# A graph attention kernel: deviation by Ln and Exp from one table set, and another split of the neighbour rows over the engines

## The chip, the cores and the metric

The kernel runs on one core of one Trainium2 chip. The core has TensorE (PE), VectorE (DVE), ScalarE (ACT), GpSimd (POOL) and the DMA queues, of which SP's and POOL's are used most here. Each engine takes its instructions in order; the engines wait for each other through semaphores. The time is device microseconds per execution. The kernel before takes 5428.85 us, the median of 3 runs (5423.94 to 5437.06).

## The reference

Two graph attention layers over 10,000 nodes and 170,000 edges (each node also has a loop of its own), each with layer norm and a residual, and one more layer norm at the end, all in float32:

```python
def gat_conv(x, edge_index, W, a_src, a_dst, bias, heads, out_ch, concat):
    ...
    xl = (x @ W).reshape(n, heads, out_ch)
    alpha_src = jnp.einsum('nhc,hc->nh', xl, a_src)
    alpha_dst = jnp.einsum('nhc,hc->nh', xl, a_dst)
    e = jax.nn.leaky_relu(alpha_src[src] + alpha_dst[dst], 0.2)
    m = jax.ops.segment_max(e, dst, num_segments=n)
    e = jnp.exp(e - m[dst])
    s = jax.ops.segment_sum(e, dst, num_segments=n)
    alpha = e / (s[dst] + 1e-16)
    out = jax.ops.segment_sum(xl[src] * alpha[:, :, None], dst, num_segments=n)
    ...
def layer_norm(x, g, b):
    ...
    return (x - mu) * jax.lax.rsqrt(var + LN_EPS) * g + b
h = layer_norm(gat_conv(x, ..., W1, ..., HEADS, HID, True), g1, be1)
h1 = jax.nn.relu(h) + (x @ Wr1 + br1)
h = layer_norm(gat_conv(h1, ..., W2, ..., 1, OUT_DIM, False), g2, be2)
y = h + (h1 @ Wr2 + br2)
x = _layernorm(x + y)
```

Layer 1 has 4 heads of 256 columns, layer 2 one head of 768.

## The kernel before

First it computes x @ W1 for all 79 tiles of 128 nodes, writes it to a table in memory, one row of 1033 numbers a node, and sorts the nodes by their number of neighbours meanwhile. `TURNS` is the order in which the sorted tiles are worked: first every other tile from few neighbours to many, then back. So a tile has `SLOTS[t]` rows, from 8 up to 27 and one of 41 in the middle, and down to 9. A "row" in this text is such a slot: for each of the tile's 128 nodes one neighbour's table row, gathered by one POOL DMA into a ring in SBUF (29 rows in layer 1, 41 in layer 2).

**Layer 1** (`ordered_layer1`, L679) works tile by tile, in an order written out by hand:

- `logits` (L472) adds and subtracts on DVE and takes Exp on ACT (L486), for all rows of a tile; `normalised` (L493) divides by the sum on DVE. `weights_of` (L733) issues both, the next tile's while this tile is still being summed (the last `EARLY` = 5 rows, later where the ring is too small; for tiles of 24 rows or more only after the tile).
- The rows are summed by their weights in three ways. The first `on_pe(t)` rows go to PE: ACT makes a diagonal matrix for each head (L722), PE multiplies it with the row (L728). Every `SHARE`-th of the others is multiplied and added by DVE alone (four instructions, L520). The rest are shared: ACT multiplies in place (L509, four instructions, `multiply`), DVE adds (L516, one instruction).
- The diagonals of a tile are issued in two halves, two rows and the remaining ones; between them ACT's order has the deviation of the tile before.
- `deviation` (L569) takes the mean and variance on DVE (L573, L575) and a Sqrt on ACT (L577). `scaled` (L580) takes the reciprocal (L588) and scales on DVE (L586, L589); L799 adds the residual.
- PE turns x and h (L700), ACT copies both out of PSUM (L701), PE multiplies with Wr1 (L172) and W2 (L816), ACT copies the result for layer 2's table (L758).
- ACT's multiplies of a tile are issued ahead of DVE's sums, and all of them before the next tile's Exp.

**Layer 2** (`ordered_layer2`, L869) sums the first 512 columns of every row on DVE (L520) and the last 256 on PE (diagonals L928, matmuls L929), adds the residual product (L940, L943), and takes two norms a tile in `norms` (L948), the second with a reciprocal of its own (L956) and an Identity on ACT (L960). POOL writes the output (L962).

Sqrt and Exp are in different table sets, so the compiler puts an ACT_TABLE_LOAD before a Sqrt that follows an Exp and before an Exp that follows a Sqrt. There is a third path, `general_path`, for graphs that do not fit; it does not run here.

Of the kernel before, what the change touches and what calls it, by code (L numbers as in the profile page):

```python
# [31 lines left out]
AF = mybir.ActivationFunctionType  # L32
# [17 lines left out]
EARLY = 5  # L50
DIAGONALS = 5
ON_PE2 = 512
SHARE = 4
ON_PE1 = 4


# [24 lines left out]
def gnn_kernel(ctx, tc, x, x_cols, src, dst, src_col, dst_col, W1, a_src1, a_dst1, b1, g1, be1, Wr1, br1,  # L81
               W2, a_src2, a_dst2, b2, g2, be2, Wr2, br2, out, n_edges):
    nc = tc.nc
# [12 lines left out]
    SLOTS = CAPS  # L96
# [34 lines left out]
    eps = consts.tile([P, 1], F32, name="eps")  # L131
# [391 lines left out]
    def attend_parts(small, ring, acc, h_, ad, bias, heads, dh, t, summed=None):  # L523
# [7 lines left out]
        for lo, hi in zip(cuts, cuts[1:]):  # L531
# [25 lines left out]
            for q in range(lo, hi):  # L557
                shared = heads > 1 and (q - lo) % SHARE
                if shared:
# [5 lines left out]
    def pieces(a, width):  # L565

        return [a[:, c:c + width] for c in range(0, a.shape[1], width)]

    def deviation(small, parts):  # L569

        st = small.tile([P, len(parts), 6], F32, name="st")
        for j, a in enumerate(parts):
            nc.vector.bn_stats(st[:, j, :], a)  # L573
        mv = small.tile([P, 2], F32, name="mv")
        nc.vector.bn_aggr(mv, st.rearrange("p k s -> p (k s)"))  # L575
        sd = small.tile([P, 1], F32, name="sd")
        nc.scalar.activation(sd, mv[:, 1:2], AF.Sqrt, bias=eps)  # L577
        return mv[:, 0:1], sd

    def scaled(to, parts, mean_and_deviation, g, b):  # L580

        mean, inv = mean_and_deviation
        c = 0
        for a in parts:
            d = c + a.shape[1]
            nc.vector.scalar_tensor_tensor(to[:, c:d], a, mean, g[:, c:d], op0=OP.subtract, op1=OP.mult)  # L586
            c = d
        nc.vector.reciprocal(inv, inv)  # L588
        nc.vector.scalar_tensor_tensor(to, to, inv, b, op0=OP.mult, op1=OP.add)  # L589

    def load(s, w):
# [82 lines left out]
    SLOTS, FIRST = [SLOTS[t] for t in TURNS], [FIRST[t] for t in TURNS]  # L674

    def nodes(t):
        return order[:, TURNS[t]:TURNS[t] + 1]

    def ordered_layer1():  # L679
        with tc.tile_pool(name="b1", bufs=1) as pool, tc.tile_pool(name="small1", bufs=2) as small, \  # L680
                tc.tile_pool(name="ps_acc1", bufs=2, space=PSUM) as ps_acc, \
                tc.tile_pool(name="ps_h1", bufs=2, space=PSUM) as ps_half, \
# [30 lines left out]
            def on_pe(t):  # L713


                return min(max(SLOTS[t] // 2 - 5, 1), ON_PE1, SLOTS[t])

            def summed(acc, diagonals, e, q, lo, hi, m):

# [25 lines left out]
            def shared(t, k):  # L745
                return (k - on_pe(t)) % SHARE > 0

# [19 lines left out]
            for t in range(NT + 1):  # L767
                live, events = t < NT, []
                n = SLOTS[t] if live else 0
                first = done = on_pe(t) if live else 0  # L770
                whole = live and n <= ring.size

# [7 lines left out]
                if last:  # L780
                    r_before, means = last
                    stats = deviation(small, pieces(means[:, :C1], BANK))
# [13 lines left out]
                if last:  # L796
                    h = pool.tile([P, C1], F32, name="h")
                    scaled(h, [means[:, :C1]], stats, g1_b, be1_b)
                    nc.vector.scalar_tensor_tensor(h, h, 0.0, r_before[:, :C1], op0=OP.max, op1=OP.add)  # L799
# [69 lines left out]
    def ordered_layer2():  # L869
        nonlocal ps_big  # L870
        with tc.tile_pool(name="b2", bufs=1) as pool, tc.tile_pool(name="small2", bufs=2) as small, \
# [76 lines left out]
            def norms(t, h, r, means):  # L948

                stats = deviation(small, [a for m in means for a in pieces(m, C2 - ON_PE2)])  # L950
                yield
                scaled(h, means, stats, g2_b, be2_b)
                nc.vector.tensor_add(h, h, r[:, :C2])
                mean, inv = deviation(small, pieces(h, C2 // 2))
                yield
                nc.vector.reciprocal(inv, inv)  # L956
                less = small.tile([P, 1], F32, name="less")
                nc.vector.scalar_tensor_tensor(less, mean, -1.0, inv, op0=OP.mult, op1=OP.mult)
                o = pool.tile([P, C2], F32, name="out")
                nc.scalar.activation(o, h, AF.Identity, bias=less, scale=inv)  # L960
                yield
                nc.gpsimd.indirect_dma_start(  # L962
                    out=out, out_offset=bass.IndirectOffsetOnAxis(ap=nodes(t), axis=0),
                    in_=o, in_offset=None, bounds_check=N - 1, oob_is_err=False)
# [7 lines left out]
            for t in range(NT):  # L972
# [4 lines left out]
                if not whole(t):  # L977
# [3 lines left out]
                    nc.vector.tensor_add(ad, ring.slot(FIRST[t])[:, C2:C2 + H2], lift)  # L981
                    attend_parts(small, ring, h, h, ad, b2_b, H2, DH2, t)
                    last = norms(t, h, rs[t], [h])
                else:
                    e = (ready or list(weights_of(t)))[0]
# [22 lines left out]
                    if not t:  # L1008
                        nc.vector.tensor_add(be2_b, be2_b, adds[1])
                        nc.vector.tensor_add(be2_b, be2_b, q[:, :C2])  # L1010
                    last = norms(t, h, rs[t], [acc, rs[t][:, C2:2 * C2 - ON_PE2]])
                if t + 2 < NT and t + 2 not in ins:
                    ins[t + 2] = fetch_x(t + 2)
# [220 lines left out]
    with tc.If(all_fits > 0) as fit:  # L1234
        ordered_layer1()
        ordered_layer2()
# [49 lines left out]
```

## Time and profile before

| | |
|---|---|
| Median of 3 runs | 5428.85 us |
| Profiled execution, its own time | 5437.06 us |
| Its span | 5435.3 us |
| Mean granted TensorE clock | 0.94 |
| PE busy | 4792.7 us, 88% |
| DVE busy | 4311.7 us, 79% |
| ACT busy | 3150.6 us, 58% |
| POOL busy | 3225.8 us, 59% |
| DMA | 1591.40 MB, 293 GB/s over the span |

The page cuts the span into 40 equal slices of 136 us. One digit is the busy share in tenths, 9 for 90% or more:

```profile
PE   8999996999999886578999999999998775789998
DVE  5784244889988887688889998779988767789998
ACT  3434344788888877678888877534443332334443
PEclk9999998999999988789999999999998887889999
DMA  4333626899999997689999998599999988999995
```

The first seven slices are the table and the sorting, the next 19 layer 1, the rest layer 2. The dip in the middle of each layer is the stretch of tiles with many rows. ACT is busiest in layer 1, where it does the multiplies. A share of busy time is a mean over a stretch; whether an engine has room is read from the order of its instructions and what each waited for. In the timelines the columns are start, duration, engine, line, operation, tile written and tiles read, their shapes, the number of instructions merged into the line, and in brackets the idle time before it with what ended it.

### The profile page before, as it was taken

To read this page: it belongs to the slowest core of one execution; us is meant where nothing else is said; L and a number is where in the kernel's file an instruction comes from. 1 tells how busy PE (TensorE), PEld (TensorE's weight loads), DVE (VectorE), ACT (ScalarE), POOL (GpSimd) and SP (SyncE) were. 2 spreads that over 40 slices of the span, in tenths; PEclk is the share of its full clock that TensorE was granted. 3 is DMA by queue.
4 is the path that set the end of the run, shared out by engine and by line. 5 is a ranking of instruction groups with operands and counts; after the bars stand their busy time and mean duration, and the time that the engine had idled before them with its cause. 6 is when DMAs were issued, how large, how long until landed. Compare 5 with 4: busy or idle time off the path is not lost. (4 is left out here: it accounts for less than half of the span.)

```text
span 5435.3 us, 59962 instructions
## 1 busy us (share of the span) xinstructions
PE 4792.7 (88%) x15191; PEld 2873.3 (53%) x15191; DVE 4311.7 (79%) x7966; ACT 3150.6 (58%) x8255; POOL 3225.8 (59%) x3159
## 2 busy tenths in 40 slices
PE   8999996999999886578999999999998775789998
PEld 3444443555555544345555555566666554566665
DVE  5784244889988887688889998779988767789998
ACT  3434344788888877678888877534443332334443
POOL 3446465455665654556656655277777657677774
PEclk9999998999999988789999999999998887889999
DMA  4333626899999997689999998599999988999995
GB/s 155 124 96 90 95 92 232 288 317 346 356 348 341 349 330 283 235 318 346 352 337 347 353 335 305 178 376 378 374 363 353 325 274 306 332 348 366 369 384 216
DMA packets 474309, 1591.40 MB, mean 293 GB/s; under 512 B 118327, under 2 KB 122487, under 8 KB 473958
## 3 DMA queue, kind: packets, MB, share of 16 engines
q0 software_dynamic: 322384, 1286.62, 65.5%
q1 hardware_dynamic: 149520, 297.43, 15.9%
q10 hardware_dynamic: 2054, 3.42, 0.2%
q8 instruction: 128, 2.10, 0.2%
q14 instruction: 223, 1.83, 0.1%
HBM read 1431.80 MB, written 177.29 MB: 296 GB/s over the span
## 5 line engine op out<-in xcount | busy, mean ns | idle before, releaser
L425 POOL DMA_INDIRECT ring<-table,slots x2675 | 2645.1, 989 | 1612.1 <-DVE acc L520 410.4
L520 DVE SCALAR_TENSOR_TENSOR acc<-ring,e,acc 128x512 f32<-128x512 f32 (+1 forms) x2530 | 1577.2, 623 | 160.4 <-PE acc L728 84.6
L509 ACT ACTIVATE ring<-ring,e 128x256 f32<-128x256 f32 x3284 | 1337.3, 507 | 0.0
L516 DVE TENSOR_TENSOR acc<-acc,ring 128x1024 f32<-128x1024 f32 x801 | 985.7, 1231 | 71.4 <-ACT ring L509 7.6
L929 PE MATMUL big<-ring,diagonals 128*128 128x256 f32 x2754 | 689.4, 413 | 206.9 <-ACT diagonals L928 186.7
L172 PE MATMUL big<-w,xT 128*128 128x512 f32 x1896 | 824.5, 597 | 22.6 <-DMA w<-in_W_dram 9.4
L172 PE MATMUL big<-wr,xT 128*128 128x512 f32 x1896 | 842.1, 601 | 0.2 <-ACT xT L701 0.2
L816 PE MATMUL half<-w,hT 128*128 128x512 f32 (+1 forms) x2528 | 830.4, 486 | 0.0
L943 PE MATMUL big<-wr,w 128*128 128x512 f32 (+1 forms) x2464 | 821.7, 486 | 0.0
L929 PEld LDWEIGHTS big<-ring,diagonals 128*128 128x128 f32 x2754 | 566.6, 208 | 327.0 <-ACT diagonals L928 228.2
L728 PE MATMUL acc<-ring,diagonals 128*128 128x256 f32 x1912 | 497.1, 419 | 244.7 <-ACT diagonals L722 244.7
L816 PEld LDWEIGHTS half<-w,hT 128*128 128x128 f32 x2528 | 477.7, 189 | 372.8 <-issue 311.2
L943 PEld LDWEIGHTS big<-wr,w 128*128 128x128 f32 x2464 | 469.2, 190 | 328.9 <-issue 297.0
L172 PEld LDWEIGHTS big<-w,xT 128*128 128x128 f32 x1896 | 361.6, 191 | 481.1 <-issue 462.7
L172 PEld LDWEIGHTS big<-wr,xT 128*128 128x128 f32 x1896 | 360.4, 194 | 425.8 <-issue 425.1
L728 PEld LDWEIGHTS acc<-ring,diagonals 128*128 128x128 f32 x1912 | 400.0, 212 | 333.0 <-ACT diagonals L722 267.2
L577 ACT ACTIVATE sd<-mv,eps 128x1 f32<-128x1 f32 x237 | 69.7, 294 | 837.9 <-DVE mv L575 831.5
L928 ACT ACTIVATE diagonals<-ident,e 128x128 f32<-128x128 f32 x1377 | 411.5, 387 | 138.8 <-DVE e L500 124.8
L661 DVE TENSOR_TENSOR scr<-big,ad_b 128x1024 f32<-128x1024 f32 x79 | 96.7, 1224 | 374.9 <-ACT row L658 374.9
L722 ACT ACTIVATE diagonals<-ident,e 128x128 f32<-128x128 f32 x956 | 292.1, 387 | 114.5 <-DVE e L500 114.2
L666 POOL TENSOR_TENSOR row<-row,none 128x1024 f32<-128x1024 f32 x79 | 187.2, 2369 | 260.3 <-ACT row L658 259.8
L664 ACT ACTIVATE scr<-scr 128x256 f32<-128x256 f32 x632 | 253.5, 402 | 120.3 <-DVE scr L661 120.3
(174 smaller groups left out, 3790.1 us busy)
## 6 DMA issues: line engine op xcount, KB each, us to landing
ring<-table,slots POOLq DMA_INDIRECT x2675, 6.9
table<-row SPq DMA_DIRECT2D x79, 516.0 KB, 3.5
h_d<-hT SPq DMA_DIRECT2D x79, 512.0 KB, 6.8
w<-h_d SPq DMA_DIRECT2D x77, 512.0 KB, 8.4
table<-row SPq DMA_DIRECT2D x79, 385.0 KB, 6.2
ring<-table SPq DMA_DIRECT2D x79, 385.0 KB, 6.6
xT<-in_x_cols_dram SPq DMA_DIRECT2D x79, 384.0 KB, 4.4
x_d<-xt SPq DMA_DIRECT2D x79, 384.0 KB, 6.7
```

What stands on the lines that cost most here:

```text
L172: nc.tensor.matmul(p[:, c:e], aT[:, j, :], w[:, j, c:e], start=(j == 0), stop=(j == k - 1))
L425: nc.gpsimd.indirect_dma_start(out=to, out_offset=None, in_=table, in_offset=bass.IndirectOffsetOnAxis(ap=index, axis=0), **more)
L509: nc.scalar.activation(row[:, s], row[:, s], AF.Copy, scale=e[:, h:h + 1])
L516: nc.vector.tensor_add(acc[:, :c], acc[:, :c], row[:, :c])
L520: nc.vector.scalar_tensor_tensor(acc[:, s], row[:, s], e[:, h:h + 1], (acc if first is None else first)[:, s], op0=OP.mult, op1=OP.add)
L664: nc.scalar.activation(m[:, s], m[:, s], AF.Copy, accum_out=row[:, C1 + i * H1 + h:C1 + i * H1 + h + 1])
L722: nc.scalar.activation(diagonals[:, k * H1 + i, :], ident, AF.Copy, scale=e[:, k, i:i + 1])
L728: nc.tensor.matmul(acc[:, c:d], diagonals[:, k * H1 + i, :], ring.slot(q + k)[:, c:d], start=(k == 0 and c % BANK == 0), stop=(k == m - 1 ...
L816: nc.tensor.matmul(q, hT[:, j, :], w2[:, j, c:c + q.shape[1]], start=(j == 0), stop=(j == K1 - 1))
L928: nc.scalar.activation(diagonals[:, k % G, :], ident, AF.Copy, scale=e[:, k, :])
L929: nc.tensor.matmul(to, diagonals[:, k % G, :], ring.slot(FIRST[t] + k)[:, ON_PE2:C2], start=False, stop=(k == n - 1), skip_group_check=True)
L943: nc.tensor.matmul(r[:, c:d], hT[:, j, :], wr2[:, j, c:d], start=False, stop=(j == K1 - 1 and (d < C2 or not whole(t))), skip_group_check= ...
```

## The change

The deviation becomes exp(-0.5 ln(var + eps)): an Ln and an Exp on ACT take the place of a Sqrt on ACT and a reciprocal on DVE, in layer 1 and in both norms of layer 2. One table load at the head of layer 1 names a set that has Ln and Exp. `SHARE` goes from 4 to 8: one row in eight, not one in four, of those that PE does not take is left to DVE alone. `on_pe` gives PE one row fewer for tiles of 14 to 19 rows (2, 3 or 4 rows become 1, 2 or 3), and the same as before for shorter and longer ones.

```diff
-SHARE = 4
+SHARE = 8
...
-        nc.scalar.activation(sd, mv[:, 1:2], AF.Sqrt, bias=eps)
+        nc.scalar.activation(sd, mv[:, 1:2], AF.Ln, bias=eps)
+        nc.scalar.activation(sd, sd, AF.Exp, scale=-0.5)
         return mv[:, 0:1], sd
...
-        nc.vector.reciprocal(inv, inv)
         nc.vector.scalar_tensor_tensor(to, to, inv, b, op0=OP.mult, op1=OP.add)
...
     def ordered_layer1():
+        nc.scalar.add_instruction(mybir.InstLoadActFuncSet(name=nc.get_next_instruction_name(), act_func_set_id=6, engine=nc.scalar.engine))
...
-                return min(max(SLOTS[t] // 2 - 5, 1), ON_PE1, SLOTS[t])
+                return min(max(SLOTS[t] // 2 - 6, 1), ON_PE1, SLOTS[t])
...
-                nc.vector.reciprocal(inv, inv)
                 less = small.tile([P, 1], F32, name="less")
```

The change's description also names "x stored when it lands" and "next softmax at another row". The lines that do these (L689, where x is stored, and L852, which sets the row) are the same in both kernels.

## The prediction

> **What bounds the kernel now.** I first read the busy time in four stretches: the three parts of layer 1 (tiles with up to 19 rows, tiles with 20 or more, tiles with up to 19 again), and layer 2. Columns: stretch, its length, busy time (instructions) of PE, weight loads, DVE, ACT, POOL, then granted clock, DMA share, GB/s.
>
> ```profile
> 925.70:1755.70 830.00, 770.23 (x2544) 455.16 (x2544) 730.25 (x1219) 660.56 (x1611) 475.21 (x468) 0.98 0.93 334
> 1755.70:2689.70 934.00, 715.43 (x2308) 443.40 (x2308) 763.23 (x1227) 713.59 (x1799) 533.31 (x528) 0.88 0.86 314
> 2689.70:3500.60 810.90, 755.45 (x2478) 443.77 (x2479) 720.03 (x1191) 648.91 (x1582) 433.27 (x428) 0.98 0.88 316
> 3500.60:5435.30 1934.70, 1689.89 (x5855) 1149.17 (x5853) 1600.81 (x3313) 758.58 (x1856) 1329.76 (x1377) 0.92 0.92 338
> ```
>
> In the first and third stretch PE is 93% busy, DVE 88%, ACT 80%. By shares ACT has room. The timeline of one tile of 17 rows says otherwise. First ACT, whole:
>
> ```profile
> 1464.63 0.29 ACT L577 ACTIVATE sd<-mv,eps 128x1 f32<-128x1 f32 x1 [3.54 <-DVE mv L575]
> 1464.83 1.26 ACT L722 ACTIVATE diagonals<-ident,e 128x128 f32<-128x128 f32 x4
> 1466.00 0.83 ACT L758 COPY row<-half 128x512 f32<-128x512 f32 x2
> 1466.73 1.71 ACT L509 ACTIVATE ring<-ring,e 128x256 f32<-128x256 f32 x4
> 1468.34 0.84 ACT L701 COPY xT<-half 128x512 f32<-128x512 f32 x2
> 1469.07 3.31 ACT L509 ACTIVATE ring<-ring,e 128x256 f32<-128x256 f32 x8
> 1472.27 1.06 ACT L701 COPY hT<-half 128x512 f32<-128x512 f32 x2
> 1473.22 11.30 ACT L509 ACTIVATE ring<-ring,e 128x256 f32<-128x256 f32 x28
> 1484.54 1.28 ACT L486 ACT_TABLE_LOAD   x1
> 1485.83 0.26 ACT L486 ACTIVATE e<-e 128x68 f32<-128x68 f32 x1
> 1487.44 2.46 ACT L722 ACTIVATE diagonals<-ident,e 128x128 f32<-128x128 f32 x8 [1.35 <-DVE e L500]
> 1489.92 1.28 ACT L577 ACT_TABLE_LOAD   x1
> 1494.72 0.29 ACT L577 ACTIVATE sd<-mv,eps 128x1 f32<-128x1 f32 x1 [3.52 <-DVE mv L575]
> ```
>
> From one deviation (1464.63) to the next Exp (1485.83) ACT has no gap. It works in order, so the Exp of the next tile stands behind every multiply of this tile. And DVE waits for that Exp:
>
> ```profile
> 1486.13 0.23 DVE L503 TENSOR_SCALAR e<-e,loops 128x4 f32<-128x4 f32 x1 [0.64 <-ACT e L486]
> ...
> 1487.26 2.49 DVE L516 TENSOR_TENSOR acc<-acc,ring 128x1024 f32<-128x1024 f32 x2
> 1489.79 2.06 DVE L520 SCALAR_TENSOR_TENSOR acc<-ring,e,acc 128x256 f32<-128x256 f32 x4
> 1491.89 1.23 DVE L516 TENSOR_TENSOR acc<-acc,ring 128x1024 f32<-128x1024 f32 x1
> ```
>
> After it DVE normalises, adds this tile's last four rows and forms mv, for which the next deviation on ACT waits (3.52). So the period is a loop: ACT from deviation to Exp, A = 21.2 us, then DVE from Exp to deviation, B = 8.9; 30.1 together, and no overlap between the two. ACT's idle time lies in B, where it cannot run ahead. Read tile by tile, the same holds in most tiles of 12 to 18 rows (at 15 rows DVE and ACT arrive together).
>
> A by its parts, start to start: deviation 0.20; each row of diagonals behind it 1.17; copies 0.73 + 0.73 + 0.95 = 2.41; each shared row (four multiplies at 0.403) 1.61; last multiply's end to Exp 1.41, of which the table load is 1.28. With s shared rows and d rows of late diagonals: 0.20 + 1.17d + 2.41 + 1.61s + 1.41 + 8.9. For 13 rows (s 9, d 0) that gives 27.4, measured 27.3; 16 rows (9, 1) 28.6, measured 28.5; 18 rows (10, 2) 31.4, measured 31.3.
>
> **The change, part by part.** *One table set.* In the built order 309 loads become one, ahead of layer 1. On the loop only the Exp's load counts: -1.41 per tile. The deviation's load lies in B's idle time (1489.92, then 3.52 of waiting): nothing in tiles that follow the loop. The extra Exp on sd has no row. Below, it is issued like its neighbour, 0.20; above, both run to their end with a gap, 0.29 + 0.29 + 0.10 - 0.20 = 0.48. I take 0.32 (Ln runs out at 0.29, then 0.23 until the next issue); 51 tiles times the difference is -6 to +8. The Exp waits for Ln; behind it stand the row copies and the next multiply, so this is on the loop. DVE needs sd only after L586 (1.28), which hides it. DVE's reciprocals (0.15 and a gap of 0.04) go.
>
> The Trainium skill, "ScalarE: Activation LUTs", section "What ACT_TABLE_LOAD costs", gives 1283 ns for the load, as here, and 1380 ns of drain beside it, about 2.66 us a switch. The trace has 1.41 from multiply to Exp and no such drain. By the page's figure each of 51 tiles would save 1.25 more, an estimate of -64, which would turn the sum below from +21 into -43.
>
> *Shares.* A DVE-only row (L520 x4) costs DVE 2.16 start to start, a shared row DVE 1.31 and ACT 1.61, a PE row ACT 1.17 and PE 1.87 (16 matmuls for two rows, 3.73). Tiles of 14 to 19 rows lose one PE row. Shared rows per tile, before to after: 12 rows 8 to 9, 13 rows 9 to 10, 14 rows 9 to 11, 15 and 16 rows 9 to 12, 17 and 18 rows 10 to 13, 19 rows 11 to 14, 20 and 21 rows 12 to 14, 22 rows 13 to 15. In all 182 more, as in the built order (728 multiplies more, 172 diagonals fewer). From 14 rows on, the last four rows hold no DVE-only row any more: B falls by 0.8 to 8.1.
>
> New loop, 0.20 + 0.32 + 1.17d + 2.41 + 1.61s + B, against the measured means: 12 rows 26.3 (25.87), 13 rows 27.9 (27.80), 14 rows 28.7 (28.18), 15 rows 30.35 (28.26), 16 rows 30.35 (28.59), 17 rows 31.95 (30.18), 18 rows 33.1 (31.59), 19 rows 34.6 (34.36). Times the tile counts 3, 5, 6, 8, 7, 8, 7, 7: 1.3 + 0.5 + 3.1 + 16.7 + 12.3 + 14.2 + 10.6 + 1.7 = **+60**. What goes is ACT's table time (1.41); what comes is three shared rows (4.8) less one late row of diagonals (1.2).
>
> *PE* gains 1.87 a tile where it is not the limit any more; it will idle longer, and in the second stretch such idling goes with a granted clock of 0.88 and with ACT waiting 1.4 to 2.2 for PE before its xT copy. In tiles of 18 and 19 rows late diagonals remain, so this may reach the loop: 0 to 1.6 for 14 tiles, 0 to +22. I take **+4**: with one late row left the transposes end about when ACT asks for them.
>
> *Tiles of 20 rows and more.* The ring of 29 rows puts the next softmax late, and ACT waits for DVE's logits (3 to 5 us for 21 to 23 rows), so extra multiplies fit in. The chain is: PE's sums, DVE's rows, logits, Exp, normalise, diagonals, PE. For 22 rows: two DVE-only rows fewer, -1.7; load -1.3; ACT's 3.2 more multiplies nearly fill its wait, so Exp comes 2.8 earlier, and of that 0.5 is lost because DVE's next row ends after it: -2.3. For 21 rows -1.8 likewise, for 23 rows -3. From 24 rows nothing is prepared ahead and DVE waits 1.34 on Exp: load -1.3, rows -1.7, -3 each. 20 rows: the loop with three last rows gives 34.6 against 34.8, nothing. Sum: 4 x 1.8 + 4 x 2.3 + 2 x 3 + 5 x 3 + 1.5 (the tile of 41) = **-39**. Bounds -25 (ACT late) to -55 (PE's wait goes too).
>
> *Layer 2.* ACT is 39% busy and its loads lie in waits for mv. The two reciprocals are 0.38 with gaps. In its 28 tiles of up to 15 rows DVE has only 0.9 idle, its gaps, so up to -10; but the DMA share there is about 1.0, so perhaps 0. Tiles of 16 rows are held by POOL (16 issues at 1.25 are 20.0, the period 19.9), larger ones wait for gathers. I take **-4**.
>
> The costs by group, which set the prices above:
>
> ```profile
> L577 ACT ACT_TABLE_LOAD x155 | 198.9, 1283 | 11.6 <-DVE mv L575 8.9
> L486 ACT ACT_TABLE_LOAD x154 | 197.6, 1283 | 98.8 <-DVE slots L489 50.6 <-DMA ring<-table,slots 27.0 <-DVE e L485 18.7
> ```
>
> Sum: 60 + 4 - 39 - 4 = **+21**. The profiled execution took 5437.06 (span 5435.3 and 1.8 around it), 8 above the median; on the median 5428.85 it gives **5450**.
>
> **Rivals.** *DVE sets the pace* (faster). For it: DVE idles only 2.2 to 2.4 of 30 in tiles of 15 to 17 rows. Then 37 tiles of 15 to 19 rows save two rows at 2.16 less three at 1.31 (0.4), a reciprocal (0.2) and the wait at L503 (about 0.5): -40; with -39 and -4 that is 5346. Against it: the wait at L503 itself. It decides if A is not filled by the multiplies. *The two sides cancel*: the loop's Exp and sd cost 0.27 less a tile than taken (51 x 0.27 = 14) and the long tiles gain 50: 60 - 14 - 50 - 4 = -8, 5421. For it: most prices are near the bounds of single rows; against it: the old loop's sum meets the measured periods to 0.1. *More than forecast* (slower; for it the xT waits above, against it the PE row that goes): PE's lower clock reaches all 14 tiles of 18 and 19 rows (+22 for +4) and the long tiles gain 30 only: +48, 5477. *It does not do what it says*: loads kept inside the loop; the built order has none. The x store (L689) and the softmax's row (L852), which the change's title names, are not in the diff and move nothing.
>
> **The numbers.** Forecast 0.60, its own range 5434 to 5464 (the long tiles' bounds, -16 and +14). DVE pace 0.13, cancel 0.12, more 0.15. One measurement tells 0.2%, 10.9 us. The forecast's low end, below 5440, counts as no change (0.07). Slower: 0.53 + 0.15 = 0.68. Same: 0.07 + 0.07 from the cancel case, 0.14. Faster: 0.13 + 0.05, 0.18. The range 5408 to 5474 takes in the cancel case and half of the last, and leaves out about 0.18.
>
> **What will show it.** Right: no gap on ACT from Ln to Exp in tiles of 15 to 19 rows, periods of 30.35 at 15 and 16 rows, DVE's wait at L503 above 1 us; first and third stretch longer by about 32 each, second shorter by about 39, layer 2 within 10. Wrong: DVE not waiting at L503, or the first stretch not longer than 830; a late xT copy would show the third rival.

## The result and the profile after

The changed kernel takes 5469.28 us, the median of 4 runs (5466.7 to 5473.77); the kernel before, measured beside it, 5426.4 (4 runs, 5422.5 to 5437.06). The ratio is 1.0077, with an interval of 1.0059 to 1.0094: slower by 0.8%, 42.9 us. The forecast was 5450, slower, with a range of 5408 to 5474.

The profiled execution took 5470.37 (span 5468.6). The same four stretches as before, cut at the same deviations, first the busy times. Columns as above: stretch, length, busy time (instructions) of PE, weight loads, DVE, ACT, POOL, granted clock, DMA share, GB/s.

```profile
928.00:1785.50 857.50, 754.71 (x2366) 434.56 (x2367) 719.27 (x1071) 674.42 (x1770) 477.59 (x469) 0.95 0.90 324
1785.50:2709.70 924.20, 714.47 (x2312) 442.24 (x2310) 727.85 (x1071) 734.99 (x1959) 531.68 (x528) 0.88 0.87 318
2709.70:3548.10 838.40, 744.42 (x2309) 424.22 (x2310) 709.47 (x1046) 663.60 (x1740) 432.71 (x428) 0.95 0.86 305
3548.10:5468.60 1920.50, 1679.18 (x5857) 1141.74 (x5855) 1584.97 (x3154) 587.30 (x1859) 1325.30 (x1377) 0.93 0.92 341
```

| stretch | before | after | difference | forecast |
|---|---|---|---|---|
| up to layer 1 | 925.7 | 928.0 | +2.3 | 0 |
| first (up to 19 rows) | 829.9 | 857.5 | +27.6 | +32 |
| second (20 rows and more) | 934.1 | 924.1 | -10.0 | -39 |
| third (up to 19 rows) | 810.9 | 838.4 | +27.5 | +32 |
| layer 2 | 1934.7 | 1920.5 | -14.2 | -4 |

In the first and third stretch every engine is busy for less of the time than before, PE's clock went from 0.98 to 0.95, and the time grew: nothing is overloaded, the engines wait for one another more. ACT's busy time rose by only 14 to 15 us a stretch: the table loads that left (two a tile, 28 tiles, 1.28 each: 72 us) nearly pay for the multiplies that came.

A tile of 17 rows after the change, ACT from one deviation to the next (line numbers behind L577 are mostly one higher than before):

```profile
1484.38 0.29 ACT L577 ACTIVATE sd<-mv,eps 128x1 f32<-128x1 f32 x1 [4.07 <-DVE mv L575]
1484.71 0.20 ACT L578 ACTIVATE sd<-sd 128x1 f32<-128x1 f32 x1
1484.82 0.84 ACT L759 COPY row<-half 128x512 f32<-128x512 f32 x2
...
1493.63 14.49 ACT L509 ACTIVATE ring<-ring,e 128x256 f32<-128x256 f32 x36
1507.99 0.27 ACT L486 ACTIVATE e<-e 128x68 f32<-128x68 f32 x1
1509.55 2.44 ACT L723 ACTIVATE diagonals<-ident,e 128x128 f32<-128x128 f32 x8 [1.29 <-DVE e L500]
1516.06 0.29 ACT L577 ACTIVATE sd<-mv,eps 128x1 f32<-128x1 f32 x1 [4.07 <-DVE mv L575]
```

And DVE at the end of the same tile:

```profile
1504.42 1.21 DVE L516 TENSOR_TENSOR acc<-acc,ring 128x1024 f32<-128x1024 f32 x1
1508.30 0.23 DVE L503 TENSOR_SCALAR e<-e,loops 128x4 f32<-128x4 f32 x1 [2.67 <-ACT e L486]
...
1509.43 5.03 DVE L516 TENSOR_TENSOR acc<-acc,ring 128x1024 f32<-128x1024 f32 x4
1515.82 0.21 DVE L575 BATCH_NORM_AGGREGATE mv<-st 128x2 f32<-128x12 f32 x1
```

From Ln (1484.38) to Exp (1507.99) ACT has no gap, 23.6 us; DVE has finished what it can and waits 2.67 for that Exp (0.64 before); then comes DVE's part to the next Ln, 8.07 with ACT idle for 4.07 of it. Together 31.7; 30.1 before. The second instruction on sd costs the loop 0.24 (what follows starts 0.44 after the Ln; after the Sqrt it was 0.20).

The groups of ACT's multiplies and DVE's additions on the page, columns count, busy time, mean ns, idle time before and what ended it:

```profile
L509 ACT ACTIVATE ring<-ring,e 128x256 f32<-128x256 f32 x4012 | 1637.3, 510 | 0.0
...
L516 DVE TENSOR_TENSOR acc<-acc,ring 128x1024 f32<-128x1024 f32 x983 | 1209.5, 1230 | 143.1 <-ACT ring L509 78.7
```

Before, it was 3284 multiplies, and DVE's additions idled 71.4, of which 7.6 for the multiplies. DVE now waits for ACT at a place where it hardly did.

### The profile page after: what moved, and what is told of

Its sections match the earlier page's. It is cut to its first block, busy times and chain, and to the rows that moved or that the text cites. A ratio compares the mean times of both kernels' runs of the same rounds, so it can differ in the third digit from the quotient of the medians.

```text
span 5468.6 us, 59040 instructions
## 1 busy us (share of the span) xinstructions
PE 4758.0 (87%) x14847; PEld 2825.8 (52%) x14847; DVE 4238.6 (78%) x7355; ACT 3030.9 (55%) x8740; POOL 3220.5 (59%) x3159
## 5 line engine op out<-in xcount | busy, mean ns | idle before, releaser
L509 ACT ACTIVATE ring<-ring,e 128x256 f32<-128x256 f32 x4012 | 1637.3, 510 | 0.0
L520 DVE SCALAR_TENSOR_TENSOR acc<-ring,e,acc 128x512 f32<-128x512 f32 (+1 forms) x1974 | 1306.1, 662 | 128.0 <-PE acc L729 71.1
L516 DVE TENSOR_TENSOR acc<-acc,ring 128x1024 f32<-128x1024 f32 x983 | 1209.5, 1230 | 143.1 <-ACT ring L509 78.7
L172 PE MATMUL big<-wr,xT 128*128 128x512 f32 x1896 | 865.9, 615 | 0.2 <-ACT xT L702 0.2
L729 PE MATMUL acc<-ring,diagonals 128*128 128x256 f32 x1568 | 421.4, 428 | 252.7 <-ACT diagonals L723 252.7
L577 ACT ACTIVATE sd<-mv,eps 128x1 f32<-128x1 f32 x237 | 69.6, 294 | 977.0 <-DVE mv L575 972.5
L172 PEld LDWEIGHTS big<-wr,xT 128*128 128x128 f32 x1896 | 371.6, 200 | 440.6 <-issue 439.9
L729 PEld LDWEIGHTS acc<-ring,diagonals 128*128 128x128 f32 x1568 | 333.9, 217 | 333.1 <-ACT diagonals L723 277.5
L929 ACT ACTIVATE diagonals<-ident,e 128x128 f32<-128x128 f32 x1377 | 411.2, 387 | 143.0 <-DVE e L500 118.4
L486 ACT ACTIVATE e<-e 128x68 f32<-128x68 f32 (+29 forms) x160 | 38.3, 239 | 480.4 <-DVE e L485 453.4
```

The lines of the kernel that those rows point to most:

```text
L172: nc.tensor.matmul(p[:, c:e], aT[:, j, :], w[:, j, c:e], start=(j == 0), stop=(j == k - 1))
L509: nc.scalar.activation(row[:, s], row[:, s], AF.Copy, scale=e[:, h:h + 1])
L516: nc.vector.tensor_add(acc[:, :c], acc[:, :c], row[:, :c])
L520: nc.vector.scalar_tensor_tensor(acc[:, s], row[:, s], e[:, h:h + 1], (acc if first is None else first)[:, s], op0=OP.mult, op1=OP.add)
L729: nc.tensor.matmul(acc[:, c:d], diagonals[:, k * H1 + i, :], ring.slot(q + k)[:, c:d], start=(k == 0 and c % BANK == 0), stop=(k == m - 1 ...
L929: nc.scalar.activation(diagonals[:, k % G, :], ident, AF.Copy, scale=e[:, k, :])
```

## The experiments

Each run below is read by its stretches of layer 1, cut as above, since layer 2 can't be compared between sessions: in the session of the result and of the last run the kernel before took 5426, in the three others 5729 to 5754, and the difference lies almost wholly in layer 2 (1921 to 1935 us against 2204 to 2248 in the kernels profiled). Ratios are to the kernel before in the same session. The stretches are those of one profiled execution each.

The first stretch has a part that goes by the session too. Its first tile, of 10 rows, took 28.6 to 31.5 us in the session of the result and of the last run and 21.4 to 24.5 in the others, whichever the kernel; in the kernel before ACT waits 8.69 there for PE ahead of its xT copy, in e1_tables not at all. So the column "12 to 19 rows", the sum over the 51 tiles that the forecast counts, is the one to compare between sessions.

Where tiles are alike in several kernels, they show the scatter: the second stretch is 923.1 to 928.2 in five kernels with one table set, one row of eight for DVE alone and no other edit there; the 51 tiles are 1568.6 and 1570.2 in two kernels alike there (the changed kernel and e9_spread).

| kernel | first | second | third | first + third | 12 to 19 rows | ratio (interval) |
|---|---|---|---|---|---|---|
| before | 829.9 | 934.1 | 810.9 | 1640.8 | 1514.5 | 1 |
| after | 857.5 | 924.1 | 838.4 | 1695.9 | 1568.6 | 1.0077 (1.0059 to 1.0094) |
| e1_tables | 802.4 | 929.6 | 786.0 | 1588.4 | 1471.4 | 0.9894 (0.9859 to 0.9930) |
| e2_share | 873.7 | 944.8 | 861.6 | 1735.3 | 1614.5 | 1.0209 (1.0168 to 1.0250) |
| e3_pe | 837.9 | 933.2 | 825.0 | 1662.9 | 1543.1 | 1.0044 (1.0027 to 1.0060) |
| e4_tables_share | 844.2 | 923.1 | 832.3 | 1676.5 | 1556.8 | 1.0030 (1.0013 to 1.0047) |
| e5_load_before_exp | 889.1 | 939.2 | 873.9 | 1763.0 | 1638.5 | 1.0188 (1.0163 to 1.0213) |
| e6_load_before_ln | 853.6 | 926.3 | 840.5 | 1694.1 | 1572.8 | 1.0052 (1.0033 to 1.0070) |
| e7_early | 862.4 | 925.3 | 848.7 | 1711.1 | 1588.5 | 1.0082 (1.0061 to 1.0104) |
| e9_spread | 850.7 | 916.1 | 837.7 | 1688.4 | 1570.2 | 1.0045 (1.0029 to 1.0060) |
| e10_apart | 827.4 | 927.2 | 812.7 | 1640.1 | 1522.9 | 0.9965 (0.9952 to 0.9979) |
| e11_apart_pe | 821.7 | 928.2 | 799.6 | 1621.3 | 1504.1 | 0.9921 (0.9898 to 0.9944) |
| e12_apart_tables | 808.5 | 928.2 | 790.6 | 1599.1 | 1483.8 | 0.9902 (0.9876 to 0.9928) |
| e13_mixed | 799.8 | 917.9 | 770.5 | 1570.3 | 1445.9 | 0.9829 (0.9816 to 0.9842) |

### The parts of the change, one by one

Four kernels, each with some of the three parts.

**e1_tables**: the change without its shares; only Ln, Exp and the one table load are left.

```diff
-SHARE = 8
+SHARE = 4
...
-                return min(max(SLOTS[t] // 2 - 6, 1), ON_PE1, SLOTS[t])
+                return min(max(SLOTS[t] // 2 - 5, 1), ON_PE1, SLOTS[t])
```

> The Ln and Exp with the one table load alone; shares as before (SHARE 4, PE's rows as before). Loop theory: the loop of a tile loses the load's 1.41 and gains the second Exp's 0.24, -1.17, and where that goes below them DVE's or PE's own work takes over: 13 rows 26.2 us, 15 rows 27.7, 17 rows 29.5, 18 rows 30.5. First and third stretch together 35 to 45 us shorter than before. Tiles of 20 to 23 rows: unchanged, since DVE does another row while the load runs; tiles of 24 and more 1.3 less each; layer 2 10 to 14 less. Total about 5370 us, ratio 0.985 to 0.992. Rival (DVE or PE sets the pace, the loads were idle time): ratio 0.996 to 1.0, only layer 2's gain.

Measured 0.9894; first and third -52.4, the 51 tiles -43.1. In tiles of 15 to 18 rows DVE no longer waits on the Exp: at most 0.1 at L503, where it was up to 0.2 before at 15 rows, 0.1 to 0.6 at 16 and 17, and 0.8 to 1.4 at 18. In a tile of 15 rows DVE runs through from its rows to the division:

```profile
1229.03 1.01 DVE L520 SCALAR_TENSOR_TENSOR acc<-ring,e,acc 128x256 f32<-128x256 f32 x2
1229.96 0.22 DVE L503 TENSOR_SCALAR e<-e,loops 128x4 f32<-128x4 f32 x1
```

and ACT waits for DVE's mv:

```profile
1238.53 0.29 ACT L577 ACTIVATE sd<-mv,eps 128x1 f32<-128x1 f32 x1 [4.91 <-DVE mv L575]
```

So one table set alone moves the tiles of 16 to 18 rows from the loop to DVE's own pace (16 rows 28.1 for 28.6, 17 rows 29.5 for 30.2, 18 rows 30.3 for 31.6); at 15 rows, where DVE hardly waited before, it gains 0.2. That is the rival "DVE sets the pace", and it is what the table set would have brought without the shares.

**e2_share**: the kernel before, with `SHARE = 8` alone. **e3_pe**: the kernel before, with PE's row alone taken away. Their edits, in this order:

```diff
-SHARE = 4
+SHARE = 8
```

```diff
-                return min(max(SLOTS[t] // 2 - 5, 1), ON_PE1, SLOTS[t])
+                return min(max(SLOTS[t] // 2 - 6, 1), ON_PE1, SLOTS[t])
```

> The kernel before with SHARE 8 alone, Sqrt and its loads as before. Loop theory: 12 and 13 rows 1.6 us longer (one shared row more), 15 to 18 rows 2 to 2.4 longer (two shared rows more, 3.2, less 0.8 for the last four rows): periods about 28.9, 29.7, 30.9, 32.5 and 33.7 us for 13, 15, 16, 17 and 18 rows. First and third stretch together 70 to 85 us longer, the long tiles -10 to +5; ratio 1.012 to 1.016. Rival (DVE sets the pace): a little faster, 0.995 to 1.0.

> The kernel before with one PE row fewer at 14 to 19 rows alone (SHARE 4). Loop theory: a shared row more (1.6 us) for a late row of diagonals less (1.2) at 16 to 19 rows, +0.4; 15 rows +0.6; at 14 rows the row goes to DVE and PE has less, -0.5. Together -5 to +10 us, ratio 0.998 to 1.002. Rival (PE sets the pace): 1.9 less in 43 tiles, ratio 0.985.

e2_share cost more than was expected, 1.0209: first and third +94.5, the 51 tiles +100.0, second +10.7. e3_pe too, 1.0044: first and third +22.1, the 51 tiles +28.6. The loop's sum has 0.4 a tile for it at 16 rows; measured are 29.7 for 28.6. The reason shows in a tile of 16 rows of e3_pe, first ACT, then DVE:

```profile
1352.21 1.28 ACT L486 ACT_TABLE_LOAD   x1 [0.60 <-DVE e L485]
1353.79 0.23 DVE L503 TENSOR_SCALAR e<-e,loops 128x4 f32<-128x4 f32 x1
```

ACT waits 0.60 for DVE's logits, and DVE does not wait on the Exp any more (at most 0.3 at 16 rows, 0.1 to 0.6 before). So DVE's own work sets the pace there: the shared row costs it 1.31, and its wait of 0.3 on average took up only a part of that.

**e4_tables_share**: the change with PE's rows as before.

```diff
-                return min(max(SLOTS[t] // 2 - 6, 1), ON_PE1, SLOTS[t])
+                return min(max(SLOTS[t] // 2 - 5, 1), ON_PE1, SLOTS[t])
```

> The changed kernel with PE's rows as before: one table set and SHARE 8. Loop theory: the periods of SHARE 8 alone less 1.17: about 27.7, 28.5, 29.7, 31.3 and 32.5 us for 13, 15, 16, 17 and 18 rows. First and third stretch together about 20 us longer than before (the changed kernel: 55), long tiles -10, layer 2 -14: ratio 0.997 to 1.001. So the row taken from PE would be the dearest part of the change, although by itself it costs nothing. Rival (the parts simply add up): as the changed kernel, within 5 us, 1.007.

1.0030, between the two figures that were expected; first and third +35.7, the 51 tiles +42.3. Against e2_share this differs by the table set alone: -57.7 over 51 tiles, 1.13 a tile, close to the loop's price for it (1.41 saved, 0.24 added by the second instruction on sd, 1.17).

The parts do not add up. Over the 51 tiles they are -43.1 (tables) + 100.0 (shares) + 28.6 (PE) = +85.5, and the whole is +54.1. The table set saves more where the loop binds (57.7 with the new shares) than alone, where DVE's own pace stops the gain, and PE's row costs less behind the other two (11.8, the changed kernel against e4_tables_share) than alone. In the second stretch the sum is -4.5 + 10.7 - 0.9 = +5, measured -10: the new shares cost 10.7 there with the loads in place and gain 6.5 without them (e4_tables_share against e1_tables).

### What a load costs, and where

**e5_load_before_exp** and **e6_load_before_ln**: the changed kernel with one load put back, at one of the two places where loads were before.

```diff
+        if not ring.own:
+            nc.scalar.add_instruction(mybir.InstLoadActFuncSet(..., act_func_set_id=6, ...))
         nc.scalar.activation(e, e, AF.Exp)
```

```diff
+                    nc.scalar.add_instruction(mybir.InstLoadActFuncSet(..., act_func_set_id=6, ...))
                     stats = deviation(small, pieces(means[:, :C1], BANK))
```

> The changed kernel with one table load put back just ahead of layer 1's Exp on the logits, 79 loads, nothing else. Theory (loop: what stands on ACT between one deviation and the next Exp counts in full, 1.28 to 1.41 us a load): 51 tiles of 12 to 19 rows longer by 1.28 to 1.41 each, so the first and third stretch together +65 to +72 over the changed kernel (1695.9); tiles of 20 to 23 rows about 0, because DVE still has a row of its own (2.0 us) to do between its logits and the division, which hides the load; the six longer tiles +1.3 each, so the second stretch (924.1) +5 to +10. Rival 1 (a table load costs 2.66 us, as a page of the notes has it): first and third +136. Rival 2 (ACT's order is not on the path): within 10 of the changed kernel. Rival 3 (the forecast's price for the long tiles was right and something else ate it): second stretch +25 or more.

> The changed kernel with one table load put back ahead of every deviation of layer 1, where ACT waits for DVE's mv (3.5 us in a tile of 17 rows), 79 loads, nothing else. Theory (the load of the deviation lay in ACT's idle time, so its removal is worth nothing in tiles that follow the loop): first and third stretch within 8 of the changed kernel's 1695.9, the second within 8 of 924.1. Rival (every load counts where it stands, 1.28 us): first and third +65, second +28.

Ahead of the Exp: first and third +67.1, the 51 tiles +69.9 (+68.3 against e9_spread, alike there and of the same session). Tiles of 12 to 17 rows rise by 1.45 on average (15 rows 31.54 for 30.05, 17 rows 33.17 for 31.67), those of 18 and 19 rows by 1.15; at 18 rows ACT's gaps between deviation and Exp shrink from 0.60 to 0.15 at the same time. A tile of 15 rows in e5_load_before_exp, ACT (line numbers two higher by the edit):

```profile
1249.64 1.32 ACT L511 ACTIVATE ring<-ring,e 128x256 f32<-128x256 f32 x3
1250.98 1.28 ACT L487 ACT_TABLE_LOAD   x1
1252.27 0.25 ACT L488 ACTIVATE e<-e 128x60 f32<-128x60 f32 x1
```

and DVE:

```profile
1252.56 0.23 DVE L505 TENSOR_SCALAR e<-e,loops 128x4 f32<-128x4 f32 x1 [3.89 <-ACT e L488]
```

The load starts 0.02 after the last multiply's end and lasts 1.28, and the Exp starts 1.31 after that end. In the changed kernel the Exp starts 0.13 before the last multiply has ended (1507.99, against 1493.63 + 14.49). So the load costs 1.44 on ACT, 0.16 more than it lasts. Ahead of the Ln: first and third -1.8, second +2.2, 15 rows 30.11 for 30.05; the 51 tiles are +4.2 against the changed kernel and +2.6 against e9_spread, hardly beyond the scatter. The same instruction, 79 times each, costs some 70 over the 51 tiles at one place and next to nothing at the other.

The Trainium skill, "ScalarE: Activation LUTs", section "What ACT_TABLE_LOAD costs", has about 2.66 for every switch to a different set, by an estimate 136 for the 51 tiles. No run here shows that. The load of e5_load_before_exp names the set that is active already; but in the kernel before, where the sets do change, the Exp starts 1.31 after the last multiply's end as well (1485.83, against 1473.22 + 11.30), and taking these changes out saved 1.13 a tile (e4_tables_share against e2_share).

The second stretch rose by 15.1 with the load ahead of the Exp, where +5 to +10 was expected: in the six tiles of 20 rows DVE does reach the division early enough to wait (0.8 to 4.0 us there); over the stretch its idle time at the division is 15.1, against 3.0 in the changed kernel.

### Moving the softmax

**e7_early** asks for the next tile's softmax four rows earlier. **e10_apart** does the same, but leaves the division at its old row.

```diff
-                    begin = max(n - EARLY, n + SLOTS[t + 1] - ring.size + EARLY)
+                    begin = max(n - 9, n + SLOTS[t + 1] - ring.size + EARLY)
...
-                    if begin <= k < begin + 2:
+                    if k in (begin, max(begin + 1, n - EARLY)):
```

The first line is in both, the second in e10_apart alone.

> The changed kernel with the next tile's softmax asked for when nine rows of this tile are left instead of five (later where the ring is too small, as before), so that part of this tile's multiplies stands behind the Exp on ACT and is worked off while DVE divides and adds. Theory (period = ACT from deviation to Exp plus DVE from Exp to deviation, no overlap): the overlap takes multiplies out of the first term, so periods fall towards ACT's own sum or DVE's: 13 rows 27.7 to about 26, 14 rows 28.4 to about 27, 15 rows 30.0 to about 28.3, 16 rows 30.1 to about 29; first and third stretch together -25 to -60 against 1695.9, the wait of DVE on the Exp's result (1.8 to 2.7 us) below 1. Above 18 rows the ring keeps the old row: second stretch within 8 of 924.1. Rival 1 (ACT or PE sets the pace by its sum of work, the order does not matter): within 10. Rival 2 (the earlier logits make DVE wait for the gathers of the next tile, whose rows come free late): longer by 10 or more, with DVE waiting on DMA ahead of its logits.

e7_early was a miss: not 25 to 60 shorter, but 15.2 longer (the 51 tiles +19.9: those of up to 15 rows 5.6 shorter, those of 16 to 19 rows some 26 longer). A tile of 15 rows, ACT:

```profile
1228.26 0.27 ACT L486 ACTIVATE e<-e 128x60 f32<-128x60 f32 x1
1228.41 1.73 ACT L509 ACTIVATE ring<-ring,e 128x256 f32<-128x256 f32 x4
1230.01 1.30 ACT L723 ACTIVATE diagonals<-ident,e 128x128 f32<-128x128 f32 x4
1231.18 4.93 ACT L509 ACTIVATE ring<-ring,e 128x256 f32<-128x256 f32 x12
1242.50 0.29 ACT L577 ACTIVATE sd<-mv,eps 128x1 f32<-128x1 f32 x1 [6.39 <-issue]
```

Sixteen multiplies left ACT's part, which fell from 22.0 to 15.7. But DVE too asked four rows earlier and waited as before (2.1 at L503), and then had four rows more to add: its part rose from 8.0 to 14.2, and ACT idles 6.39 ahead of the Ln. A row counts in the loop on one side or on the other, as long as DVE takes the Exp's result right after it asked for it. At 17 rows a part is the expectation's second rival: DVE idles 7.7 in all ahead of its logits there, mostly for DMAs, and not at all in the changed kernel.

> The changed kernel with the softmax of the next tile taken apart: logits and Exp when nine rows of this tile are left (later where the ring is too small), the division by the sum and the diagonals at the fifth row from the end, where they were. The run that only moved both together to the ninth row was 15 longer in the first and third stretch, not 25 to 60 shorter: what left ACT's part of the loop (16 multiplies, 6.3 us) came back in DVE's part (8.0 to 14.2 us), and DVE still waited 2 us on the Exp. Theory (the loop is closed by DVE taking the Exp's result right after it asked for it, so a row counts either on ACT or on DVE): with the two parted DVE does four rows meanwhile and its wait (1.8 to 2.7 us) goes; 13 rows 27.7 to about 25.5, 14 rows 28.4 to 26.5, 15 and 16 rows 30.0 to about 28, 17 rows 31.7 to 31; from 18 on no change, as the ring holds the Exp behind the multiplies. First and third stretch together -40 to -75 against 1695.9, second within 8 of 924.1. Rival 1 (ACT or PE sets these tiles by its own sum): within 10. Rival 2 (the loop closes through the last multiplies and mv, which the parting does not touch): DVE's wait at L503 goes and comes back as waits on multiplies, total within 15 of 1695.9.

With the two parted, DVE does four rows between logits and division and waits for nothing. DVE in the same tile of e10_apart:

```profile
1211.67 3.88 DVE L516 TENSOR_TENSOR acc<-acc,ring 128x1024 f32<-128x1024 f32 x3
1215.59 2.06 DVE L520 SCALAR_TENSOR_TENSOR acc<-ring,e,acc 128x256 f32<-128x256 f32 x4
1217.56 0.22 DVE L503 TENSOR_SCALAR e<-e,loops 128x4 f32<-128x4 f32 x1
```

The period is 27.8 (30.1 in the changed kernel), first and third -55.8, the 51 tiles -45.7, ratio 0.9965 with the change's own shares. In tiles of up to 16 rows it is the loop, then, that made the change slower: opened, with the same work per engine, they are shorter than in the kernel before too (12 to 15 rows 585.7 in all for 611.7, 16 rows 28.3 for 28.6). At 17 rows the ring lets the Exp forward by little (30.0 to 33.0 against 31.7). At 18 rows, where no change was expected, six of seven tiles got longer (34.8 on average, 33.5 in the changed kernel): the logits came a row earlier, but the Exp still stood behind all multiplies, so DVE waits 3.3 for it instead of 2.4, and its part of the loop has a row more (9.2 for 8.1). For these tiles the loop is shown by its periods and its waits, not by opening it.

**e11_apart_pe** and **e12_apart_tables** are the same edit on e4_tables_share and on e1_tables.

> As e10_apart, with PE's rows as in the kernel before (one of eight for DVE alone, one table set, softmax parted). Against the same without the parting (first and third stretch 1676.5): -35 to -75 if the parting takes away DVE's wait on the Exp; within 15 if not. Against e10_apart: one shared row less (ACT 1.61, DVE 1.31) for one row of diagonals more (ACT 1.17) and 1.87 on PE, so -10 to -45 if ACT and DVE pace, 0 to +10 if PE does.

> The kernel before with one table set and the softmax parted as in e10_apart; a quarter of the rows for DVE alone, PE's rows as before. Without the parting DVE already set the pace there and did not wait on the Exp (first and third stretch 1588.4), so the parting should bring little: within 12 of 1588.4. If DVE's wait was only hidden among its other waits: -15 to -40.

e11_apart_pe: -55.2 against e4_tables_share (the 51 tiles -52.7), and -18.8 against e10_apart. e12_apart_tables: +10.7 against e1_tables (+12.4). There the tiles of 12 to 14 rows, in which DVE waited 0.7 to 1.2 on the Exp, got shorter by 0.6 to 0.7, and those of 15 to 19, in which it hardly waited, longer by 0.2 to 1.8. The parting helps where DVE waits on the Exp and the ring lets it come early, and nowhere else.

### The long tiles

The second stretch by DVE's groups: busy time, mean ns, idle time before. The kernel before:

```profile
L516 DVE TENSOR_TENSOR acc<-acc,ring 128x1024 f32<-128x1024 f32 x278 | 342.4, 1232 | 26.3 <-ACT ring L509 0.5
L520 DVE SCALAR_TENSOR_TENSOR acc<-ring,e,acc 128x256 f32<-128x256 f32 x408 | 199.5, 489 | 76.5 <-PE acc L728 63.2
...
L478 DVE TENSOR_TENSOR e<-ring 128x40 f32<-128x40 f32 (+18 forms) x36 | 7.1, 208 | 26.1 <-DMA ring<-table,slots 22.9 <-issue 3.2
```

The changed kernel:

```profile
L516 DVE TENSOR_TENSOR acc<-acc,ring 128x1024 f32<-128x1024 f32 x323 | 397.7, 1231 | 66.4 <-ACT ring L509 44.5 <-DVE acc L516 0.5 <-DVE acc L520 0.5
L520 DVE SCALAR_TENSOR_TENSOR acc<-ring,e,acc 128x256 f32<-128x256 f32 x228 | 111.6, 489 | 71.5 <-PE acc L729 64.3
...
L478 DVE TENSOR_TENSOR e<-ring 128x40 f32<-128x40 f32 (+18 forms) x36 | 7.2, 208 | 18.4 <-DMA ring<-table,slots 16.8 <-issue 1.5
```

DVE lost 35.4 us of work (763.2 to 727.9), about what the forecast hoped to gain. But its additions idle 40.1 more (26.3 to 66.4), nearly all for ACT's multiplies; 12.7 less idle at the two other groups and 2.5 less at L503 are left. -35.4 + 40.1 - 12.7 - 2.5 = -10.5, and the stretch is 10.0 shorter. By length, 8.8 of that lies in the six tiles of 24 rows and more, 0.9 in the ten of 21 to 23 rows and 0.2 in the six of 20. Where the new wait sits shows a tile of 22 rows, before:

```profile
2441.32 2.06 DVE L520 SCALAR_TENSOR_TENSOR acc<-ring,e,acc 128x256 f32<-128x256 f32 x4 [2.77 <-PE acc L728]
2443.49 3.91 DVE L516 TENSOR_TENSOR acc<-acc,ring 128x1024 f32<-128x1024 f32 x3
2447.43 2.06 DVE L520 SCALAR_TENSOR_TENSOR acc<-ring,e,acc 128x256 f32<-128x256 f32 x4
```

and after the change:

```profile
2499.37 2.06 DVE L520 SCALAR_TENSOR_TENSOR acc<-ring,e,acc 128x256 f32<-128x256 f32 x4 [3.81 <-PE acc L729]
2501.54 3.91 DVE L516 TENSOR_TENSOR acc<-acc,ring 128x1024 f32<-128x1024 f32 x3
2505.97 1.23 DVE L516 TENSOR_TENSOR acc<-acc,ring 128x1024 f32<-128x1024 f32 x1 [0.52 <-ACT ring L509]
2508.04 1.23 DVE L516 TENSOR_TENSOR acc<-acc,ring 128x1024 f32<-128x1024 f32 x1 [0.84 <-ACT ring L509]
2509.63 1.23 DVE L516 TENSOR_TENSOR acc<-acc,ring 128x1024 f32<-128x1024 f32 x1 [0.36 <-ACT ring L509]
2511.23 1.23 DVE L516 TENSOR_TENSOR acc<-acc,ring 128x1024 f32<-128x1024 f32 x1 [0.36 <-ACT ring L509]
2512.49 2.06 DVE L520 SCALAR_TENSOR_TENSOR acc<-ring,e,acc 128x256 f32<-128x256 f32 x4
```

With one row of four for DVE alone, ACT was a row ahead again after every three. With one of eight the first run is seven long, ACT needs 1.61 a row and has hT to copy in between, and DVE, at 1.3 a row, catches up.

**e9_spread** puts as many rows of DVE's own, in tiles of 20 rows and more, at places 0, 4 and 12 instead of 0, 8 and 16.

```diff
-                return (k - on_pe(t)) % SHARE > 0
+                if SLOTS[t] < 20:
+                    return (k - on_pe(t)) % SHARE > 0
+                return k - on_pe(t) not in ((0, 4, 12) if SLOTS[t] - on_pe(t) > 16 else (0, 4))
```

> The changed kernel; in tiles of 20 rows or more the rows that DVE does alone, as many as before, stand at places 0, 4 and 12 of its rows instead of 0, 8 and 16, so that the first run of shared rows is three long and not seven. Theory (in the long tiles the gain failed because the first seven shared rows run at ACT's 1.61 a row and DVE waits for each, 1 to 2 us a tile before the logits of the next): second stretch 924.1 shorter by 8 to 25, DVE's wait on ACT's multiplies there below half. Rival 1 (PE's sums at a lower clock set the long tiles, and DVE's place is slack): second stretch within 6. Rival 2 (the wait for ACT moves to the later run, of seven to ten rows, with the same total): within 6, with the wait on multiplies as large as before but later in the tile. First and third stretch as in the changed kernel.

The second stretch is 916.1, 8.0 less than in the changed kernel (6.3 of it in the tiles of 21 to 23 rows) and 7 below the lowest of the five alike; it sits at the small end of what was expected. The same two groups of e9_spread there:

```profile
L516 DVE TENSOR_TENSOR acc<-acc,ring 128x1024 f32<-128x1024 f32 x323 | 397.7, 1231 | 42.6 <-ACT ring L509 12.0 <-issue 5.6 <-DVE acc L516 0.6
...
L478 DVE TENSOR_TENSOR e<-ring 128x40 f32<-128x40 f32 (+18 forms) x36 | 7.4, 209 | 30.6 <-DMA ring<-table,slots 26.7 <-issue 3.9
```

The idle time at the additions fell by 23.8, and half of that came back ahead of the logits (18.4 to 30.6): coming earlier, they wait for the gathers of the next tile's rows. So the wait on ACT's first run took a part of the gain away, and behind it the gathers stand as the next limit. That it took all of it is not shown: the stretch is still 21 above the forecast's 895.

### The version put together

**e13_mixed**: one table set, PE's rows as before, and by a tile's length: up to 15 rows one of eight for DVE alone and the softmax parted; 16 to 19 rows one of four and the softmax in one piece; from 20 rows as in e9_spread.

```diff
-                return min(max(SLOTS[t] // 2 - 6, 1), ON_PE1, SLOTS[t])
+                return min(max(SLOTS[t] // 2 - 5, 1), ON_PE1, SLOTS[t])
...
-                return (k - on_pe(t)) % SHARE > 0
+                if SLOTS[t] < 20:
+                    return (k - on_pe(t)) % (8 if SLOTS[t] < 16 else 4) > 0
+                return k - on_pe(t) not in ((0, 4, 12) if SLOTS[t] - on_pe(t) > 16 else (0, 4))
...
-                    begin = max(n - EARLY, n + SLOTS[t + 1] - ring.size + EARLY)
+                    begin = max(n - (9 if n < 16 else EARLY), n + SLOTS[t + 1] - ring.size + EARLY)
...
-                    if begin <= k < begin + 2:
+                    if k in (begin, max(begin + 1, n - EARLY if n < 16 else 0)):
```

> The version put together from the runs: one table set; PE's rows as in the kernel before; tiles of 16 to 19 rows with a quarter of the rows for DVE alone and the softmax in one piece; tiles of up to 15 rows with one of eight for DVE alone and the softmax parted; tiles of 20 rows and more with DVE's own rows at places 0, 4 and 12. If each stretch takes over what the single runs gave: first and third together 1588.4 less about 8 (13 rows 26.1 to 25.6, 14 rows 26.6 to 26.0, 15 rows 27.8 to 27.0), so 1575 to 1590; second 912 to 922; ratio to the kernel before 0.984 to 0.991, a little better than one table set alone (0.9894). If the parts disturb each other at the seams between the tile lengths: first and third above 1600, ratio above 0.992.

5336.58 us, the median of 5 runs (5329.59 to 5339.4), beside 5426.38 for the kernel before: 0.9829 (0.9816 to 0.9842), 89.8 us faster than before, and beyond the range expected: first and third together came to 1570.3, 5 below it (the tiles of 12 to 15 rows 571.5, 24.7 less than in e1_tables, where about 8 was expected), and the total that the ratio divides by is shorter here, beside 5426 and not 5729 to 5754. Its three stretches of layer 1:

```profile
925.90:1725.70 799.80, 765.95 (x2552) 454.35 (x2552) 714.97 (x1144) 619.49 (x1654) 475.50 (x470) 0.99 0.95 347
1725.70:2643.60 917.90, 716.12 (x2308) 443.65 (x2308) 728.18 (x1070) 735.38 (x1959) 533.53 (x528) 0.88 0.87 320
2643.60:3414.10 770.50, 739.64 (x2478) 435.26 (x2479) 703.58 (x1109) 610.76 (x1627) 433.07 (x428) 1.00 0.91 332
```

PE is 96% busy in the first and third at a clock of 0.99 to 1.00: by this, an estimate, what is left to gain there by order alone is some 4%.

## Why the prediction was right, and where it was off

- **The loop** (A on ACT from deviation to Exp, B on DVE from Exp to deviation, no overlap): right. Both signs asked for are in the trace: no gap on ACT in tiles of 15 to 17 rows and in most of 18 and 19, and a wait at L503 of 1.8 to 2.7 in all tiles of 15 to 19 rows but one. The periods came out 0.1 to 0.3 below the forecast: 13 rows 27.7 (27.9), 14 rows 28.4 (28.7), 15 and 16 rows 30.1 (30.35), 17 rows 31.7 (31.95), 18 rows 32.9 where PE is in time (33.1), 19 rows 34.5 (34.6). By tiles that is +54, by stretches +55, for +60 and +4. Part of the difference is the second instruction on sd, taken at 0.32 and measured at 0.24. That the loop is the cause and not only a fit is shown by e5_load_before_exp and e6_load_before_ln (the same load costs about 1.45 a tile in A and less than 0.1 in B) and, for tiles of up to 16 rows, by e10_apart (parted, the loss goes).
- **PE's lower clock** (+4): about right. The xT copy was late in three tiles of 18 rows and two of 19 (34.5 for 32.9, 35.4 for 34.5), some 6 in all, not in all 14 as the third rival had it; the clock fell to 0.95.
- **The tiles of 20 rows and more** (-39, bounds -25 to -55): this is the term that was mis-sized; it measured -10, outside its bounds. The step that failed is "ACT's 3.2 more multiplies nearly fill its wait, so Exp comes 2.8 earlier". The wait was at the end of the tile, the multiplies came at its head, ahead of DVE's additions: the saved 35.4 of DVE's work was paid back as 40.1 of waiting for ACT. In the tiles of 22 rows ACT does idle less between deviation and Exp, 2.4 for 6.6, but the Exp comes 33.5 after the deviation for 33.8 (means of four), 0.3 earlier and not 2.8. The tiles of 21 to 23 rows were to give 22 and gave 0.9; those of 24 and more 16.5, and gave 8.8. The step was read from ACT's idle time in a tile and not from the order of rows within it. The load on the Exp, priced at 1.3 in these tiles, is hidden in most tiles of 21 to 23 rows (no wait at L503 with the load put back) but not in those of 20.
- **Layer 2** (-4, 0 to -10): measured -14.2 between the two profiled executions. The kernel before's profiled run was the longest of its four, 10.7 above their median, and if that lies in layer 2 the gain is 4. e13_mixed, with the same layer 2 as the changed kernel, gives the like: 89.8 less by the medians, 86.7 of it in layer 1 by the profiles. How much layer 2 gained stays open between 3 and 14.
- **The sum**: +21 forecast, +42.9 by the medians, +33.3 between the profiled executions. Of the 22 missing, the long tiles are 29; the first and third stretch, 9 lower than forecast, go the other way, by luck. The measured 5469 lies outside the forecast's own range, 5434 to 5464, and inside the wide one only.
- **The rivals**: "DVE sets the pace" did not come, but is what e1_tables does in tiles of 15 to 18 rows, and e3_pe at 15 to 17, with DVE hardly waiting at L503. "The two sides cancel" had the long tiles at -50; they gave a fifth. "More than forecast" (5477) was nearer in time than the forecast, and had one cause half right, the long tiles, which gained even less than its 30; its other cause, PE's lower clock in all 14 tiles, did not come.
- **The size of a load**: weighed in the prediction at 1.41 against 2.66. Measured at 1.44 in the run made for it. The 1.41 counts from where a next multiply would have started; from the last multiply's end to the Exp the trace has 1.31.

## What to carry to other kernels

Where two engines hand a tile back and forth, add up the chain from hand-over to hand-over in the order of their queues: work taken off one engine pays only if it leaves that chain, and moving a request and its use together only moves rows from one side of the chain to the other; parting them opens it, where the buffers let the request come early enough. Work added to an engine that idles must fit at the place where it is put in its queue, not only in its idle time per tile. And a bundle of parts should be tried part by part: here one table set alone made the kernel faster by 1.1%, and the shares that came with it took that and more. The costs of the parts alone need not add up, since each can move the limit to another engine.

## What the runs showed of the hardware that had not been expected

- After 7.42 us without work PE took 10.05 us for the 32 multiplications with diagonals of a tile of 22 rows (2489.29 in the changed kernel, granted clock 0.71 over that time); in the kernel before, after 8.57 us, it took 9.18 (2432.10, clock 0.78). Running on, four rows take 7.5 (1.87 a row). DVE's first row waits 3.81 for them. The long tiles' PE sums thus pay for PE's own waiting.
- The same program took 6% longer in three sessions, nearly all of it in layer 2: e9_spread's layer 2 moved 296 GB/s at a DMA share of 0.84 in 2211 us, the changed kernel's 341 GB/s at 0.92 in 1920. Layer 1 was alike to within 1% there. The cause was not looked for.
- A table load in a row of ACT instructions costs more than its own 1.28: without it the Exp starts 0.11 to 0.13 before the multiply ahead of it has ended, with it 1.31 after, 1.42 to 1.44 later.
- In layer 2 the second instruction on sd does not come free: DVE's last scaling (L589) idles 21.2 for 2.8 before, 13.1 of it for the Exp on sd; before, the reciprocal idled 16.7 for the Sqrt, so the two are nearly even.
